# Layer 1 of a four-layer image network in one lane with fixed turns, beside the attention of layer 0

## The chip, the core and the metric

The kernel runs on one core of one Trainium2 chip. The core has five engines, each with its own queue that is worked off in order: PE (matrix products), DVE (vector arithmetic), ACT (activation functions and copies), POOL (a second, slower vector engine) and SP (which issues DMAs here). [...] The metric is the device time of one execution in microseconds (us), where lower is better.

## What is computed

Four layers follow each other on a batch of 4 images of 256 channels and 48 x 48 points (N = 2304). Each begins with a group norm of its input and adds its result to it:

```python
x = x + _L0_conv_ref(_gn(x), ...)   # attention: 8 heads of 64, q and k of length one
x = x + _L1_conv_ref(_gn(x), ...)   # a gate from a blurred, strip-convolved copy
x = x + _L2_conv_ref(_gn(x), ...)   # attention with one head of 64
x = x + _L3_conv_ref(_gn(x), ...)   # channel gate, 3 x 3 depthwise filter, norm
```

Layer 0 is the largest. Per image and head it forms `softmax(10 * q^T k) v` over 2304 x 2304 scores, then an output product. Layer 1 is small and has no large product:

```python
x_tem = _blur_pool(_max_pool_3x3(x), stride=3)          # 48 x 48 -> 16 x 16
s = x_h1 + x_w1 + x_h2 + x_w2                           # strip filters, 11 x 3 taps each
gate = jax.nn.sigmoid(batch_norm(s))
return x * gate[:, :, idx_h][:, :, :, idx_w]            # each gate value for 3 x 3 points
```

The four strip filters are summed into one filter per channel, whose taps the kernel lists in `TAPS`.

## The kernel before

**Tiling.** 256 channels are two tiles of 128 partitions (`k` = 0, 1; `NK` = 2). Heads are taken in pairs (`p` = 0 to 3). One head pair of one image is a phase: six units, each for 384 of the 2304 query points. A unit walks over the 18 blocks of 128 keys two at a time, so it has nine groups (`NG` = 9). The place of a group in its unit is called slot 0 to 8 below, so a phase has 54 groups and layer 0 has 16 phases, 864 groups. Layer 2 follows with 4 x 27 groups of the same kind, and layer 3 after them.

**One group.** `attend` (L382) writes the order of every engine by hand. For group t it emits: the scores of the two key blocks on PE and their exponentials on ACT (`scores`, L237 and L243; two PSUM tiles, so scores of one group need the exponentials of the one before); the sums of the exponentials of group t-1 on DVE and, for odd groups, first on POOL (`add_up`, L268, L277, L283); the jobs due in this group (`due`, then `fills`); the lanes, described below; and the value products of group t-1 on PE (`weigh`, L257). Eight buffers `pt` hold exponentials. A `pt` is free once `weigh` and `add_up` are done with it.

**What is due in a unit.** After the ninth group, in slot 0 of the next unit, `last` copies the result out of its single PSUM buffer (`take`, L330, ACT) and books the rest, counted in groups from there: the row sums (`total`, 3 groups on), a fold on POOL (2), the inverse of the sums with its DMAs (`invert`, L310 to L325, 6), the division on POOL (`divide`, L338, 10) and the output product with its addition to x (`out_proj`, L579 on PE, L584 on DVE, 11). Eleven groups on is slot 2 of the unit after. There a chunk of the next head pair's q, v and k is also made: in the order of PE, output product of the first channel half, q (L513), v (L529), k (L513), output product of the second half. They share two PSUM buffers `pj`. So v can start only when DVE has added the first output product to x, and k when ACT has moved q out. In groups 49, 51, 52 and 53 of a phase, DVE scales q for the next phase (L549 to L563).

**Layer 1 beside it.** For images 0 to 2 layer 1 runs in the phases of the next image (image b-1 beside image b), and for image 3 beside layer 2 (`l1_last`, which uses PE). Its work is a Python generator, `l1_all(b)` (L1011): group norm statistics (`gn`, L167); for each k the maxima and the blur (`maxima`, L666, six steps for each half image, DVE alone, L678 to L710); the padded tile (`padded`, L716, POOL, DVE and ACT); 19 rounds of products (`strips`, L728: four or five products on ACT, L741, and one sum on DVE, L759); the gate and its application (`gated`, L844, with POOL multiplications L867 and DVE additions L869); and the statistics for the norm of layer 2. Each `yield` ends one step. The number that it gives is how many groups to wait before the next.

A lane in `attend` spreads `n` steps evenly over its groups a to z, takes none in slot 0, and in its last group takes all that are left:

```python
until = -(-n * (st["at"] + 1 - a) // (z - a))
final = st["at"] == z - 1
while final or (done < until and t >= ready and not ends):
```

The generator is cut into four parts of 33 steps, one per phase (`part`, `L1_ALL`). The gate of k = 0 runs in a second list, `aside`, beside the maxima of k = 1.

Of the kernel before, what the change touches and what calls it, by code (L numbers as in the profile page):

```python
# [17 lines left out]
NK = 2  # L18
# [56 lines left out]
def usual_path(  # L75
# [88 lines left out]

    GN_TICKS = NSL + 4

    def gn(b, res, halves=range(NK)):  # L167

        if "st" not in res:
            res["st"] = small.tile([P, NK, NSL, 6], F32, tag="gn_st", name="gn_st")  # L170
        st = res["st"]
        for s in range(NSL if halves else 0):
            for k in halves:
                nc.vector.bn_stats(st[:, k, s, :], X[b][:, k, s * SL : (s + 1) * SL])
            yield 0
        mv = small.tile([P, NK, 2], F32, tag="gn_mv", name="gn_mv")
        for k in range(NK):
            nc.vector.bn_aggr(mv[:, k, :], st[:, k].rearrange("p s f -> p (s f)"))
        yield 3
        ps = pj_tile()  # L180
        nc.tensor.matmul(ps[:, 0:NK], lhsT=gmat, rhs=mv[:, :, 0], start=True, stop=True)
        gm = small.tile([P, NK], F32, tag="gn_gm", name="gn_gm")
        nc.vector.tensor_copy(gm, ps[:, 0:NK])
        dev = small.tile([P, NK], F32, tag="gn_dev", name="gn_dev")
        nc.vector.tensor_sub(dev, mv[:, :, 0], gm)
        sq = small.tile([P, NK], F32, tag="gn_sq", name="gn_sq")
        nc.vector.tensor_mul(sq, dev, dev)
        nc.vector.tensor_add(sq, sq, mv[:, :, 1])
        yield 2
        ps = pj_tile()  # L190
        nc.tensor.matmul(ps[:, 0:NK], lhsT=gmat, rhs=sq, start=True, stop=True)
        gv = small.tile([P, NK], F32, tag="gn_gv", name="gn_gv")
        nc.vector.tensor_scalar(gv, ps[:, 0:NK], GN_EPS, None, ALU.add)
        rs = small.tile([P, NK], F32, tag="gn_rs", name="gn_rs", bufs=6)
        rsqrt(rs, gv)
        yield 2
        nm = small.tile([P, NK], F32, tag="gn_nm", name="gn_nm", bufs=6)
        nc.vector.tensor_scalar(nm, gm, -1.0, None, ALU.mult)
        nb = small.tile([P, NK], F32, tag="gn_nb", name="gn_nb", bufs=6)
        nc.vector.tensor_mul(nb, nm, rs)  # L200
        res["rs"], res["nb"], res["nm"] = rs, nb, nm
        yield 1
# [153 lines left out]
        nc.vector.tensor_add(lsum[:, 0:1], lsum[:, 0:1], two[:, 0:1])  # L356
        nc.vector.tensor_tensor(lmin[:, 0:1], lmin[:, 0:1], two[:, 1:2], ALU.min)

    due, fills, aside, clock = {}, {}, [], {}
    AT_TOTAL, AT_FOLD, AT_INVERT, AT_DIVIDE, AT_AFTER = 3, 2, 6, 10, 11  # L360

    def last(u, t):

# [18 lines left out]
    def attend(phases):  # L382
# [16 lines left out]
        for t, (u, g, st) in enumerate(groups):  # L399
            for j in range(g * G, (g + 1) * G):  # L400
                scores(u, j)
            if prev is not None:
                add_up(*prev)
            do(due, t)
            do(fills, t)

            ends = prev is not None and prev[1] == NG - 1
            clock["t"] = t
            for lane in st["others"]:
                gen, n, a, z, done, ready = lane  # L410
                until = -(-n * (st["at"] + 1 - a) // (z - a))
                final = st["at"] == z - 1
                while final or (done < until and t >= ready and not ends):
                    wait = next(gen, None)
                    if wait is None:
                        break
                    done, ready = done + 1, t + wait
                    if final:
                        for other in list(aside):
                            if next(other[0], None) is None:  # L420
                                aside.remove(other)
                lane[4:] = done, ready
            for lane in list(aside):
                gen, ready = lane
                if t >= ready and not ends:
                    wait = next(gen, None)
                    if wait is None:
                        aside.remove(lane)
                    else:
                        lane[1] = t + max(wait, 1)  # L430
            st["at"] += 1
            if prev is not None:
                pu, pg = prev
                for j in range(pg * G, (pg + 1) * G):
                    weigh(pu, j)
                if pg == NG - 1:
                    last(pu, t)
            prev = (u, g)
# [220 lines left out]
        range(i, min(i + NT, len(TAPS))) for i in range(NT + 1, len(TAPS), NT)  # L659
    ]  # L660
    L1_BUF = (NT + 1) * AS * AS
    ROUND_TICKS = 2
    STRIP_TICKS = 2 * 6 + 2 + ROUND_TICKS * len(ROUNDS)
    GATE_TICKS = 7

    def maxima(b, k, res):  # L666

# [59 lines left out]

    def strips(b, k, norm, res):  # L728

        yield from maxima(b, k, res)  # L730
        pd = padded(k, norm, res)

        bufs = [
# [11 lines left out]
                )  # L745

        products(0)
        yield 2
        products(1)
        yield 2  # L750
        for n, taps in enumerate(ROUNDS):
            last = n == len(ROUNDS) - 1
            if n + 2 < len(ROUNDS):
# [5 lines left out]
            nc.vector.tensor_reduce(  # L759
                to, bufs[n % 3][:, :, : min(n, 1) + len(taps)], AX.X, ALU.add  # L760
            )

            for _ in range(ROUND_TICKS):
                yield 0

    TAPS_AT_ONCE = 12

# [242 lines left out]

    def l1_all(b):  # L1011

        yield from gn(b, norms1[b])
        res = {}
        yield from strips(b, 0, norms1[b], res)

        def rest():
            yield from gated(b, 0, norms1[b], res)
            norms2[b]["st"] = small.tile([P, NK, NSL, 6], F32, tag="gn_st2", name="gn_st2")
            for s in range(NSL):  # L1020
                nc.vector.bn_stats(
                    norms2[b]["st"][:, 0, s, :], X[b][:, 0, s * SL : (s + 1) * SL]
                )
                yield 1
            res["done"] = True

        aside.append([rest(), 0])
        one = {}
        yield from strips(b, 1, norms1[b], one)
        while "done" not in res:  # L1030
            yield 1
        yield from gated(b, 1, norms1[b], one)
        yield from gn(b, norms2[b], [1])

    def l1_last(b, ahead):

# [30 lines left out]
        def gates():  # L1067
            for k in range(NK):
                yield from until(res[k], "summed")
                yield from gated(b, k, norm, res[k])  # L1070
                yield from stats(k)
            yield from gn(b, norm2, [])

        return [ahead, tops(), sums(), gates()]

    L1_ALL = 2 * GN_TICKS + NK * STRIP_TICKS + GATE_TICKS
    l1 = [l1_all(b) for b in range(NX)]
    ahead = gn(B - 1, norms1[B - 1])
    lanes = l1_last(B - 1, ahead)

# [13 lines left out]
    def follow(start, slices, norm):  # L1094

        while "nb" not in norm:
            yield 1
        start()
        yield 1
        for c in range(L2C):  # L1100
# [28 lines left out]
    for i, (b, p) in enumerate(order):  # L1129
# [16 lines left out]
                work[NG * s + AT_CHUNK] = slices[s]  # L1146
        if (b, p) == (2, 0):
            for s in range(NSL):
                work.setdefault(s, []).append(lambda s=s: send(s))
                work.setdefault(s + 8, []).append(lambda s=s: receive(s))  # L1150
        if (b, p) == (0, 0):
            others.append((tap_weights(), WEIGHT_TICKS, 2, n - 2))
        if b > 0:
            ticks = -(-L1_ALL // NPAIR)
            first = AT_AFTER + 2 if p == 0 else 0
            others.append((part(l1[b - 1], ticks, p == NPAIR - 1), ticks, first, n - 2))
        if (b, p) == (B - 1, NPAIR - 1):
            others.append((part(ahead, L1_AHEAD, False), L1_AHEAD, n - L1_AHEAD - 3, n))
        if p == 1 and b + 1 < B:
# [1263 lines left out]
```

## The time and the profile before

| | |
|---|---|
| median of 10 runs | 3786.55 us (3781.2 to 3790.34) |
| the profiled execution: its own time | 3789.53 us |
| its span from first to last instruction | 3787.8 us |
| mean clock granted to PE | 0.967 of full speed |
| layer 0, image 0 (four phases, no layer 1 beside) | 52.7 to 761.6 us |
| layer 0, images 1 to 3 (layer 1 beside) | 761.6 to 3065.9 us |
| layer 2 | 3065.9 to 3516.8 us |
| layer 3 | 3516.8 to 3787.8 us |
| ACT exponentials L243, 1944 of them | 1477.1 us busy, 812 ns each |
| ACT products of layer 1, L741, 486 | 281.2 us, 752 ns each |
| DVE sums of layer 1, L759, 114 | 168.6 us, 1479 ns each |

The stages are cut at the first exponential of a phase. Busy time of an engine is the union or the sum of its instructions. A wait is put down to what ended it. The durations of a row are those of single instructions, which can overlap a little on one engine.

### The profile page before, as it was taken

What the parts mean: (1) busy time and instruction counts of PE and PEld (TensorE: products, weight loads), DVE (VectorE), ACT (ScalarE), POOL (GpSimd) and SP (SyncE); (2) the same over time, 40 slices, a digit from 0 to 9 for tenths busy, and PEclk for the clock granted to TensorE, in tenths of its full rate; (3) what the DMA queues carried; (4) which work ended last, traced back from release to release, by engine and by line L of the source; (5) the groups of instructions that cost most, each with busy time, mean ns of one, the idle gap of its engine ahead of it and who ended that gap; (6) DMA issues with size and microseconds to landing.
All of it is one profiled execution on the core that took longest, in us unless ns stands there. A gap on an engine that the chain in (4) does not pass through costs nothing.

```text
span 3787.8 us, 86425 instructions
## 1 busy us (share of the span) xinstructions
PE 3541.8 (94%) x36330; PEld 1797.1 (47%) x36330; DVE 2469.0 (65%) x3203; ACT 2360.3 (62%) x3819; POOL 1391.5 (37%) x900
## 2 busy tenths in 40 slices
PE   7999999998997999989979999899899999989685
PEld 4454555554443445544444445444444445655343
DVE  2455545566777666677686666766856677575687
ACT  5666666656774876658748766577487655555353
POOL 2333323332333333333333333333333356564242
PEclk9999999998998999999989999999899999999797
DMA  4111111110111111311111111111011100000001
GB/s 138 21 26 21 25 20 29 17 34 10 29 16 24 21 25 20 79 16 25 20 22 21 25 22 25 18 25 23 18 20 25 16 6 8 6 6 6 26 26 75
DMA packets 114591, 97.89 MB, mean 26 GB/s; under 512 B 56224, under 2 KB 111632, under 8 KB 112400
## 3 DMA queue, kind: packets, MB, share of 16 engines
q1 hardware_dynamic: 111728, 91.27, 12.7%
q8 instruction: 286, 4.69, 0.5%
q10 hardware_dynamic: 2464, 1.00, 0.1%
q14 instruction: 113, 0.93, 0.1%
HBM read 59.33 MB, written 11.80 MB: 19 GB/s over the span
## 4 chain that ended last, share of the span: by engine, by line
PE 69%; DVE 16%; ACT 7%; issue 5%; POOL 2%; DMA 1%; DVEq 0%; SPq 0%; ACTq 0%; POOLq 0%
PE sc L237 26%; PE av L257 25%; PE pj L513 6%; DVE acc L283 4%; PE pj L529 4%; PE pj L579 3%; ACT prod L741 3%; DVE sc L1413 2%; ACT pt L243 2%; DVE av L1413 1%; PE pj L290 1%; POOL half L268 1%; PE pj L805 1%; ACT row L299 1%; DVE acc L277 1%
## 5 line engine op out<-in xcount | busy, mean ns | idle before, releaser
L243 ACT ACTIVATE pt<-sc 128x768 f32<-128x768 f32 x1944 | 1477.1, 812 | 866.8 <-PE sc L237 863.3
L268 POOL TENSOR_TENSOR half<-pt 128x768 f32<-128x768 f32 x477 | 921.7, 1933 | 1818.5 <-ACT pt L243 1759.5
L237 PE MATMUL sc<-q,k 64*64 64x384 f32 x13824 | 1283.5, 486 | 36.0 <-DVE q L563 22.1
L257 PE MATMUL av<-pt,v 64*64 64x384 f32 x13824 | 1281.2, 486 | 0.0
L283 DVE TENSOR_TENSOR acc<-acc,pt 128x768 f32<-128x768 f32 x792 | 829.9, 1048 | 108.4 <-ACT pt L243 26.9
L237 PEld LDWEIGHTS sc<-q,k 64*64 64x64 f32 x13824 | 514.8, 133 | 661.3 <-issue 539.2
L257 PEld LDWEIGHTS av<-pt,v 64*64 64x64 f32 x13824 | 519.8, 133 | 588.9 <-issue 557.4
L283 DVE TENSOR_TENSOR acc<-acc,half 128x768 f32<-128x768 f32 x459 | 457.2, 996 | 416.5 <-POOL half L268 416.1
L584 DVE SCALAR_TENSOR_TENSOR x<-pj,bo,x 128x384 f32<-128x384 f32 x192 | 118.3, 617 | 564.1 <-PE pj L579 564.1
L513 PE MATMUL pj<-xs,w 128*128 128x384 f32 (+1 forms) x768 | 295.3, 510 | 2.3 <-issue 1.7
L741 ACT ACTIVATE prod<-pd,wt 128x256 f32<-128x256 f32 x486 | 281.2, 752 | 0.2
L338 POOL TENSOR_TENSOR o<-o,rinv 128x384 f32<-128x384 f32 x95 | 131.3, 1382 | 270.2 <-DMA rinv<-rinv 257.8
L529 PE MATMUL pj<-w,xs 128*128 128x128 f32 x1152 | 160.1, 293 | 41.1 <-DVE x L584 41.1
L579 PE MATMUL pj<-o,wo 128*128 128x384 f32 x384 | 169.2, 523 | 27.8 <-POOL o L338 22.9
L529 PEld LDWEIGHTS pj<-w,xs 128*128 128x128 f32 x1152 | 155.5, 207 | 75.0 <-DVE x L584 53.5
L513 PEld LDWEIGHTS pj<-xs,w 128*128 128x128 f32 x768 | 146.4, 202 | 85.7 <-issue 14.0
L257 PE MATMUL av<-pt,qv 64*64 64x384 f32 x1728 | 176.3, 502 | 0.0
L237 PE MATMUL sc<-qv,kd 64*64 64x384 f32 x1728 | 171.0, 490 | 3.9 <-ACT pt L243 3.9
L759 DVE TENSOR_REDUCE prod<-prod 128x256 f32<-128x1280 f32 x114 | 168.6, 1479 | 0.3
L277 DVE TENSOR_TENSOR acc<-pt 128x768 f32<-128x768 f32 x99 | 113.9, 1151 | 10.6 <-ACT pt L243 10.5
L579 PEld LDWEIGHTS pj<-o,wo 128*128 128x128 f32 x384 | 66.0, 193 | 112.7 <-issue 51.2
L330 ACT COPY raw<-av 128x768 f32<-128x768 f32 x108 | 86.3, 799 | 43.7 <-PE av L257 43.5
(226 smaller groups left out, 2696.9 us busy)
## 6 DMA issues: line engine op xcount, KB each, us to landing
xs<-in_x_dram SPq DMA_DIRECT2D x96, 384.0 KB
rinv<-rinv SPq DMA_DIRECT2D x208, 94.5 KB
x<-in_x_dram SPq DMA_DIRECT2D x6, 1152.0 KB
out_dram<-x SPq DMA_DIRECT2D x6, 1152.0 KB
l<-row SPq DMA_DIRECT2D x416, 1.5 KB
w<-in_wqkv_dram SPq DMA_DIRECT2D x32, 192.0 KB
rinv<-ls SPq DMA_DIRECT2D x208, 1.5 KB
x_out<-x SPq DMA_DIRECT2D x6, 384.0 KB
```

The costliest lines, as they stand in the source:

```text
L237: nc.tensor.matmul(ps[c * D : (c + 1) * D, h, :SL], lhsT=u["of"]["k"][r, j0 : j0 + D], rhs=u["of"]["q"][r, u["qc"]], start=True, stop=True,)
L243: nc.scalar.activation(pt, ps[:, :, :SL], AF.Exp, scale=u["scale"])
L257: nc.tensor.matmul(u["av"][h * D : (h + 1) * D, half, :SL], lhsT=value(u, j, h)[r], rhs=pt[r, h, :], start=j == 0, stop=j == JB - 1,)
L268: nc.gpsimd.tensor_add(half, pts[0], pts[1])
L277: nc.vector.tensor_add(u["acc"], ready[0], ready[1])
L283: nc.vector.tensor_add(u["acc"], u["acc"], term)
L338: eng.tensor_mul(o, o, u["rinv"])
L513: nc.tensor.matmul(ps[:, :n], lhsT=at["w"][:, k, t, :], rhs=xs[s][:, k, :n], start=k == 0, stop=k == NK - 1,)
L529: nc.tensor.matmul(ps[:, i * P : (i + 1) * P], lhsT=xs[s][:, k, i * P : (i + 1) * P], rhs=at["w"][:, k, 2, :], start=k == 0, stop=k == NK - 1,
L579: nc.tensor.matmul(ps[:, :SL], lhsT=wo[:, p, k * P : (k + 1) * P], rhs=o["o"], start=True, stop=True,)
L741: nc.scalar.activation(bufs[n % 3][:, :, min(n, 1) + i].rearrange("p (r c) -> p r c", c=AS), pd[:, PAD + dr : PAD + dr + AS, PAD + dc : PA ...
L759: nc.vector.tensor_reduce(to, bufs[n % 3][:, :, : min(n, 1) + len(taps)], AX.X, ALU.add)
```

## The change

Layer 1 of images 0 to 2 gets a fixed place in each unit. `paced` wraps the generator: it lets it take one step in slots 3, 5, 6 and 8 and two in slot 2, and none elsewhere. A step that says `ROUND` (a round of products) is followed by steps in slots 2, 5 and 8 alone; `HASTE` does the same with slots 2, 4, 6 and 8 and is used for image 2. The generator is no longer cut: it runs on over phases, and into the first 27 groups of the image after (`others.append((l1[b - 2], ..., 0, 3 * NG))`), beside the next image's own. Nothing is taken all at once in a phase's last group.

Within `l1_all` the order becomes serial: maxima, products and gate of k = 0, the statistics of k = 0, then the same for k = 1; the list `aside` goes. The first half of the maxima of k = 0 is taken before the norm's end. Between the blur and the padded tile at least three groups pass (`yield 3`). The rounds go on after the padded tile as before.

In layer 0 and layer 2, `invert` moves from 6 groups to 5 and `divide` from 10 to 9. The copy of image 0's x to memory and image 3's x into its place (`send`, `receive`) move from groups 0 to 5 and 8 to 13 of the phase to groups 18 to 23 and 36 to 41. `follow`, which starts the products of layer 2's last image, waits two groups more. The sums of `bn_stats` in `gn` yield after two slices where one channel half is taken. Layer 3 is as it was.

```diff
-    AT_TOTAL, AT_FOLD, AT_INVERT, AT_DIVIDE, AT_AFTER = 3, 2, 6, 10, 11
+    AT_TOTAL, AT_FOLD, AT_INVERT, AT_DIVIDE, AT_AFTER = 3, 2, 5, 9, 11
...
-            clock["t"] = t
+            clock["t"], clock["slot"] = t, st["at"] % NG
...
-                final = st["at"] == z - 1
+                clock["final"] = final = st["at"] == z - 1
...
+    TURNS, ROUND, HASTE = (2, 2, 3, 5, 6, 8), -1, -2
+    ROUND_TURNS = {ROUND: (2, 5, 8), HASTE: (2, 4, 6, 8)}
+
+    def paced(gen):
+
+        at, count, wait, turns = -9, 0, 0, TURNS
+        while True:
+            t, slot = clock["t"], clock["slot"]
+            count = count if t == at else 0
+            if not clock["final"] and (t < at + wait or count >= turns.count(slot)):
+                yield 1
+                continue
+            wait = next(gen, None)
+            if wait is None:
+                return
+            at, count = t, count + 1
+            turns = ROUND_TURNS.get(wait, TURNS)
+            yield 0
...
     def l1_all(b):
 
-        yield from gn(b, norms1[b])
+        norm, norm2 = norms1[b], norms2[b]
+        norm2["st"] = small.tile([P, NK, NSL, 6], F32, tag="gn_st2", name="gn_st2")
+        start = clock["t"]
+        ahead = gn(b, norm)
+        for _ in range(NSL - 1):
+            yield next(ahead)
         res = {}
-        yield from strips(b, 0, norms1[b], res)
...
+        tops = maxima(b, 0, res)
+        for _ in range(6):
+            yield next(tops)
+
+        while clock["t"] < start + NG + 2:
             yield 1
-        yield from gated(b, 1, norms1[b], one)
-        yield from gn(b, norms2[b], [1])
+        yield from ahead
+        yield from tops
+        for k in range(NK):
+            if k:
+                res = {}
+                yield from maxima(b, k, res)
+
+            yield 3
+            yield from strips(b, k, norm, res)
+            yield from gated(b, k, norm, res)
+            if k == 0:
+                for s in range(NSL):
+                    nc.vector.bn_stats(norm2["st"][:, k, s, :], X[b][:, k, s * SL : (s + 1) * SL])
+                    if s % 2:
+                        yield 0
+        yield from gn(b, norm2, [1])
...
         while "nb" not in norm:
             yield 1
+        yield 2
         start()
...
-                work.setdefault(s, []).append(lambda s=s: send(s))
-                work.setdefault(s + 8, []).append(lambda s=s: receive(s))
+                work.setdefault(s + 2 * NG, []).append(lambda s=s: send(s))
+                work.setdefault(s + 4 * NG, []).append(lambda s=s: receive(s))
...
         if b > 0:
-            ticks = -(-L1_ALL // NPAIR)
-            first = AT_AFTER + 2 if p == 0 else 0
-            others.append((part(l1[b - 1], ticks, p == NPAIR - 1), ticks, first, n - 2))
+            end = n - 2 if (b, p) == (B - 1, NPAIR - 1) else n + 1
+            others.append((l1[b - 1], 10**6, 2 if p == 0 else 0, end))
+        if b > 1 and p == 0:
+            others.append((l1[b - 2], 10**6, 0, 3 * NG))
```

## The prediction

> **What bounds the kernel now.** I read the page first, for the engine that carries the span.
>
> ```profile
> PE 3541.8 (94%) x36330; PEld 1797.1 (47%) x36330; DVE 2469.0 (65%) x3203; ACT 2360.3 (62%) x3819; POOL 1391.5 (37%) x900
> PE 69%; DVE 16%; ACT 7%; issue 5%; POOL 2%; DMA 1%; DVEq 0%; SPq 0%; ACTq 0%; POOLq 0%
> ```
>
> PE is busy nearly all the time, and 16% of the chain that ended last lies on DVE. Where, the table by stages tells; I cut it at the phases of layer 0. Columns: stretch, us, busy us of PE, PEld, DVE, ACT, POOL, PE's clock, DMA.
>
> ```profile
> 405.90:583.70 177.80, 177.75 (x1932) 89.56 (x1928) 90.57 (x122) 108.85 (x172) 57.95 (x38) 1.00 0.14 24
> 583.70:761.60 177.90, 177.85 (x1932) 89.57 (x1928) 95.37 (x123) 109.00 (x172) 57.97 (x38) 1.00 0.14 24
> 761.60:962.30 200.70, 188.94 (x1940) 93.99 (x1936) 133.97 (x176) 124.31 (x203) 66.32 (x40) 0.95 0.11 19
> 962.30:1152.30 190.00, 182.24 (x1936) 88.47 (x1932) 138.27 (x172) 135.61 (x226) 68.93 (x42) 0.98 0.13 22
> 1152.30:1353.50 201.20, 187.98 (x1932) 91.88 (x1928) 135.99 (x167) 138.53 (x230) 65.66 (x39) 0.96 0.14 24
> 1353.50:1534.20 180.70, 180.03 (x1940) 89.22 (x1936) 119.73 (x154) 121.49 (x198) 66.17 (x42) 1.00 0.14 24
> ```
>
> The first two rows are image 0, with no layer 1 beside: PE never idle, full clock, 177.85 us. The next four are image 1, the same PE work with layer 1 beside: PE is idle for 12, 8 and 13 us in three of them, and its clock falls with it. Images 2 and 3 repeat this (196.7, 189.5, 201.2, 180.8; 199.6, 187.9, 199.3). Yet DVE and ACT are at most 73% busy in any phase: this is a matter of order, not of capacity. Who stops PE there, the waits in that stretch tell (total, times, longest):
>
> ```profile
> PE pj L529 <- DVE x L584: 41.1, 14, 5.1
> PE pj L579 <- POOL o L338: 22.9, 11, 4.9
> PE sc L237 <- DVE q L563: 20.2, 3, 6.8
> PE sc L237 <- ACT pt L243: 11.6, 14, 1.9
> ```
>
> And the timeline shows how, DVE around one such wait:
>
> ```profile
> 1199.83 2.56 DVE L277 TENSOR_TENSOR acc<-pt 128x768 f32<-128x768 f32 x1
> 1202.31 1.50 DVE L703 TENSOR_TENSOR tf<-t 128x400 f32<-128x400 f32 x1
> ...
> 1205.59 0.29 DVE L710 SCALAR_TENSOR_TENSOR blur<-tf 128x128 f32<-128x128 f32 x1
> 1205.80 0.61 DVE L584 SCALAR_TENSOR_TENSOR x<-pj,bo,x 128x384 f32<-128x384 f32 x1
> ```
>
> L584 frees the PSUM buffer that v (L529) needs. It stood behind 3.4 us of maxima, put in slot 1, and a sum of exponentials that was late itself; PE stood for 5.1 us and then ran at half clock.
>
> **What the Trainium skill says.** "TensorE: Matmul & The Clock Gate", Part 1: PE's clock is halved after an idle window of about 3.4 us and comes back after a busy one. The trace agrees in kind: between 761 and 2890 us there are 17 half-clock stretches of 3.4 to 10.2 us, 122.9 us together, all behind gaps; but a gap of 1.9 us was enough for one. So an idle us costs more than itself: 98.1 us of idleness in these eleven phases came with 61.4 us of clock. "Perfetto Trace Analysis", DVE / Act Engine Instruction: the recorded time runs to the acknowledged write, so the records of neighbours overlap. Here four products of 745 ns took 2.1 us from start to start:
>
> ```profile
> 1047.22 2.32 ACT L741 ACTIVATE prod<-pd,wt 128x256 f32<-128x256 f32 x4
> 1049.32 1.56 ACT L243 ACTIVATE pt<-sc 128x768 f32<-128x768 f32 x2
> ```
>
> "SBUF — State Buffer", SBUF: two separate sides: a DVE operation with two SBUF inputs and one of POOL lock each other out for their whole length. It agrees with L681, 1.37 us at its fastest and 3.05 at its slowest; I use means, which hold this.
>
> **The change part by part.** *What can be won.* The eleven phases of images 1 to 3 (all but the very last) take 2889.2 - 761.6 = 2127.6 us; without layer 1 beside, 11 x 177.85 = 1956.4. The difference is 171.2. Group norm products on PE remain: the group with one takes 3.11 instead of 2.64 us, two per norm, eight norms: 8 us. So at most 163 can go. The last phase (176.7, with other products) I leave as it is: its idle time is six waits of 0.6 for ACT that the change doesn't touch.
>
> *Rounds in slots 2, 5, 8 (or 2, 4, 6, 8).* ACT per unit: 18 exponentials at 0.71 start to start 12.8, q, v, k 2.8, two rows 0.9, one copy 0.75: 17.2. Three rounds of 2.1 make 23.5, four 25.6; PE needs 29.65. After a round the next exponential starts 0.9 us late (the groups with a round are 3.48 instead of 2.59 from exponential to exponential), and a group's slack of about 1.15 takes that up by the second group. Before, rounds in slots 1, 3 and 6 did no harm: the row 1353.50 has rounds, and 0.7 us idle. New is slot 8, before the copy L330 of the single output buffer: PE waited up to 0.3 us for it, so over 38 units between 0 and 12 us. I take 0, as the copy ends about 0.2 us ahead; four rounds cost nothing either.
>
> *Gaps that go.* Maxima no longer stand in slots 0 and 1, ahead of L584: the waits L529 <- L584 and, since DVE held POOL's buffers and the inverse up, L579 <- L338 go in the main. No phase ends with all left-over steps at once: the three waits of 6.75 us for the scaling of q (L563) go.
>
> *What stays or comes, from DVE.* A step in slot 2 is written behind the second L584, which waits for PE's last product of the slot, about 7 us into it. So slot 2 hides little, and maxima start a third of a microsecond before slot 3. A full unit then has, one after the other: steps two and three 4.5 (L681, L682, L684, L688 by their means), sums of exponentials 3.2, step four 2.8, sums and inverse 3.7, step five 2.9, step six 1.4, sums 3.2, sums 3.4, a first sum 1.1, the first L584 0.6: 26.8. Slots 3 to 1 take 21.35, and v comes 3.6 after the start of slot 2: 24.95. With the 0.3 ahead, PE waits 26.5 - 24.95 = 1.6; 0.7 for clock: 2.3. As a check on the same addition, before 1196 us it gives 22.1 for a stretch that took 21.0. Seven such units in three images: 16. Two in which step one stood in slot 8 as well (2.2 more): 4.5 each, 9. In the first units of images 2 and 3 the rest of the image before shares the turns: some 5 us of statistics and additions come on top, and PE's small norm products wait for DVE too: 9.5 each, 19. Three lighter halves, 0.5 each: 1.5.
>
> *The padded tile.* In its slot ACT gets the tile (0.6) and five products behind POOL's memset (0.75) and a small DVE operation; three groups lie between it and the blur. I count exponentials 2.5 late against 1.0 allowed: 1.5 for the three k = 0, 0.2 for two k = 1 in slot 2, and 4 for image 2's second, followed by four more products in the next group: 9.
>
> *Sum of these:* 16 + 9 + 19 + 1.5 + 9 = 54.5, so layer 0 wins 163 - 55 = 108.
>
> *Inverse and division one group earlier.* In layer 0 neither engine has a sum between the old and the new place (add_up puts nothing on DVE in slot 6, nothing on POOL in slot 1), so only lane work is overtaken, and image 0 keeps its time. SP's DMAs follow at the same moment. In layer 2 DVE's inverse passes one sum; row copies and their DMA had landed by then. 0, between -3 and +3.
>
> *`follow`.* PE stood for the norm of the last image:
>
> ```profile
> 3393.97 0.98 PE L885 MATMUL pj<-gn_nb,w2c 128*128 128x1 f32 x4 [5.96 <-DVE gn_nb L200]
> ```
>
> Half clock followed for 6.8 us (3.4 lost). Two groups, over 5 us, cover nearly all; the chunks after it stay in their groups. 8 of 9.4.
>
> *send and receive* go to SP six times each, past fetches of x, in groups when image 0's x has been final for a group or more: nothing waits. The exchange is over before image 3's norm reads it, 19 groups later. 0.
>
> *Sum:* 108 + 8 = 116. The profiled execution took 3789.5: 3673.5. It lies 3 above the median, so **3670 us**.
>
> **The rivals.** *All is hidden.* DVE runs uncontended (maxima at their fastest, 1.4 for 1.9) and residual waits fall to 12: 3789.5 - 151 - 8 - 3 = 3627. For it: image 0, and that every gap has one of four causes, each addressed. Against: slot 2 is written behind L584. *DVE lag is passed on.* Each full unit leaves the next one behind, exponentials wait for `pt` as well, clocks halve: residual 100, 3715. For it: the lag of some 7 us before 1196. *Slower.* The round in slot 8 delays L330, and with one output buffer the value products stop in slot 1, in each of 38 units. To pass 3794 (0.2% above the median) it must eat 116 + 8 = 124 us, 3.3 a unit: more than a whole round of 2.1 laid bare. Priced with one whole round and half clock after it, 4 a unit, it gives 3670 + 152 = 3822. Waits for L330 of 0.3 at most speak against it. *The change doesn't do what it says:* rounds fit their turns (about 14 units per image and 24 to place them), so the end of a lane never flushes.
>
> **How the numbers follow.** Likeliest 3670: 0.65, its own range 3640 to 3700. All hidden 0.15, lag passed on 0.15, slower 0.04, no change 0.01. The range 3628 to 3710 reaches to both neighbours and takes in the bounds above. 0.2% is about what a measurement of this kernel tells from no change. Faster 0.95, same 0.01, slower 0.04.
>
> **What would show it.** By stages: phases of image 1 at 178 to 184 with clocks near 1.00; the first phases of images 2 and 3 longest. Waits L529 <- L584 down to a few of 2 us; no 6.8 for L563; L885 waiting under 1 us. Image 0 and layer 3 as before. I am wrong if PE idles in units that hold rounds alone, or waits for L330 by more than half a microsecond.

## The result, and the profile after

The changed kernel takes 3759.53 us (median of 8 runs, 3753.41 to 3761.68); the kernel before takes 3786.55 us (median of 28, 3779.23 to 3791.34). The ratio is 0.9928 with a 95% interval of 0.992 to 0.9937: 27 us faster, where 116 were forecast, and outside the range of 3628 to 3710. The profiled execution took 3769.65 us, its span is 3767.8. It is 10 us slower than the median, so what is read from this one profile below is known to some 10 us in all; by profiles the change won 20 us.

First the page of the changed kernel, the lines that answer to the two shown of before.

```profile
PE 3535.7 (94%) x36330; PEld 1782.4 (47%) x36330; DVE 2590.3 (69%) x3203; ACT 2359.4 (63%) x3819; POOL 1453.2 (39%) x900
PE 62%; DVE 25%; issue 5%; ACT 3%; POOL 2%; DMA 1%; SPq 0%; DVEq 0%; ACTq 0%; POOLq 0%
```

DVE has the same 3203 instructions, but is busy for 2590 us instead of 2469, and its share of the chain that ended last has grown from 16% to 25%. The same work takes DVE 121 us longer.

The table by stages, cut again at layer 0's phases (stretch, us, busy us of PE, PEld, DVE, ACT, POOL, PE's clock, DMA): one phase of image 0, the four of image 1, the last of image 3.

```profile
586.40:764.30 177.90, 177.85 (x1932) 89.55 (x1928) 93.50 (x122) 108.99 (x172) 58.03 (x38) 1.00 0.14 24
764.30:955.30 191.00, 182.98 (x1948) 90.78 (x1944) 142.04 (x175) 120.09 (x195) 69.59 (x40) 0.99 0.13 21
955.30:1142.10 186.80, 181.93 (x1924) 86.70 (x1920) 144.77 (x163) 138.72 (x233) 70.15 (x39) 1.00 0.14 23
1142.10:1336.70 194.60, 183.87 (x1944) 90.70 (x1940) 146.69 (x169) 122.88 (x199) 76.47 (x42) 0.98 0.13 22
1336.70:1518.50 181.80, 180.12 (x1927) 86.61 (x1920) 135.02 (x143) 137.32 (x231) 67.80 (x38) 1.00 0.14 24
...
2859.00:3045.90 186.90, 179.66 (x1908) 87.47 (x1904) 130.35 (x158) 114.42 (x175) 68.81 (x40) 0.95 0.13 21
```

Image 1 went from 200.7, 190.0, 201.2 and 180.7 to 191.0, 186.8, 194.6 and 181.8. The clock is nearly whole again (61 us were lost to it in the eleven phases of images 1 to 3, now 20), but PE's idle time in them fell only from 98 to 83 us. The very last phase went the other way, from 176.7 to 186.9. Layer 0 of images 1 to 3 as a whole: 2304.3 to 2281.6, 22.7 won where 108 were forecast.

PE's waits in that stretch (total, times, longest):

```profile
PE pj L518 <- DVE x L573: 55.8, 28, 4.5
PE sc L238 <- ACT pt L244: 9.8, 9, 2.2
PE pj L568 <- POOL o L339: 9.2, 10, 1.9
```

L518, L573, L568 and L339 are L529, L584, L579 and L338 of before. The wait of v for the first addition to x has not gone: 28 waits instead of 14, and 55.8 us instead of 41.1. The waits for the division are down from 22.9 to 9.2, the three of 6.8 for the scaling of q are gone.

To see what kind of unit pays, each unit of images 1 to 3 is taken from its slot 3 to the next slot 3, and the length of the same unit with no layer 1 (29.43 us, 30.06 in a phase's first and fifth, from image 0; 29.03 in the last phase) is taken off. The excess, by what layer 1 does in the unit, in us:

| unit holds | before | after |
|---|---|---|
| maxima | 136.6 in 15 (9.1 each) | 72.7 in 17 (4.3) |
| the padded tile | 15.9 in 6 | 14.0 in 6, three with maxima |
| rounds | 15.0 in 30 (0.50) | 32.0 in 31 (1.03) |
| a gate | 1.4 in 4 | 15.9 in 8 (2.0) |
| statistics only | 1.9 in 7 | 2.9 in 3 |
| the last phase, all six | 2.4 | 13.5 |
| sum | 173.3 | 151.1 |

A "bare" unit below is one of these lengths. The maxima paid 64 us less, as meant; rounds, gates and the last phase paid 43 us more.

### The profile page after: what moved, and what is told of

It is laid out like the page before. It is cut to its first block, busy times and chain, and to the rows that moved or that the text cites. A ratio compares the mean times of both kernels' runs of the same rounds, so it can differ in the third digit from the quotient of the medians.

```text
span 3767.8 us, 86478 instructions
## 1 busy us (share of the span) xinstructions
PE 3535.7 (94%) x36330; PEld 1782.4 (47%) x36330; DVE 2590.3 (69%) x3203; ACT 2359.4 (63%) x3819; POOL 1453.2 (39%) x900
## 4 chain that ended last, share of the span: by engine, by line
PE 62%; DVE 25%; issue 5%; ACT 3%; POOL 2%; DMA 1%; SPq 0%; DVEq 0%; ACTq 0%; POOLq 0%
PE av L258 23%; PE sc L238 23%; DVE acc L284 10%; PE pj L502 5%; PE pj L518 4%; PE pj L568 3%; DVE acc L278 2%; DVE sc L1426 2%; PE pj L291 1%; DVE av L1426 1%; ACT pt L244 1%; PE pj L809 1%; DVE gn_st L174 1%; ACT prod L747 1%; DVE x L573 1%
## 5 line engine op out<-in xcount | busy, mean ns | idle before, releaser
L269 POOL TENSOR_TENSOR half<-pt 128x768 f32<-128x768 f32 x477 | 961.4, 2017 | 1688.0 <-ACT pt L244 1619.0
L284 DVE TENSOR_TENSOR acc<-acc,pt 128x768 f32<-128x768 f32 x792 | 916.4, 1157 | 87.3 <-ACT pt L244 3.4
L284 DVE TENSOR_TENSOR acc<-acc,half 128x768 f32<-128x768 f32 x459 | 468.7, 1021 | 297.8 <-POOL half L269 295.7
L573 DVE SCALAR_TENSOR_TENSOR x<-pj,bo,x 128x384 f32<-128x384 f32 x192 | 118.1, 616 | 563.2 <-PE pj L568 563.2
L339 POOL TENSOR_TENSOR o<-o,rinv 128x384 f32<-128x384 f32 x95 | 128.4, 1352 | 303.9 <-DMA rinv<-rinv 286.7
L518 PE MATMUL pj<-w,xs 128*128 128x128 f32 x1152 | 155.9, 288 | 55.9 <-DVE x L573 55.8
L518 PEld LDWEIGHTS pj<-w,xs 128*128 128x128 f32 x1152 | 149.1, 201 | 92.3 <-DVE x L573 74.5
L568 PE MATMUL pj<-o,wo 128*128 128x384 f32 x384 | 167.7, 519 | 12.9 <-POOL o L339 9.2
L278 DVE TENSOR_TENSOR acc<-pt 128x768 f32<-128x768 f32 x99 | 140.9, 1423 | 18.6 <-ACT pt L244 18.6
L508 ACT ACTIVATE q<-pj,bias 128x384 f32<-128x384 f32 x96 | 55.7, 580 | 98.6 <-PE pj L502 97.9
L335 POOL TENSOR_TENSOR o<-raw 128x384 f32<-128x384 f32 x95 | 116.7, 1228 | 0.0
```

The costliest lines, as they stand in the source:

```text
L269: nc.gpsimd.tensor_add(half, pts[0], pts[1])
L278: nc.vector.tensor_add(u["acc"], ready[0], ready[1])
L284: nc.vector.tensor_add(u["acc"], u["acc"], term)
L518: nc.tensor.matmul(ps[:, i * P : (i + 1) * P], lhsT=xs[s][:, k, i * P : (i + 1) * P], rhs=at["w"][:, k, 2, :], start=k == 0, stop=k == NK - 1,
L568: nc.tensor.matmul(ps[:, :SL], lhsT=wo[:, p, k * P : (k + 1) * P], rhs=o["o"], start=True, stop=True,)
L573: nc.vector.scalar_tensor_tensor(xs, ps[:, :SL], pair["bo"][:, k : k + 1], xs, ALU.add, ALU.add)
```

## The experiments

All ratios are to the kernel before, run on the same chip at the same time (3787 to 3790 us in each set).

**Layer 1 left out.** How low can layer 0 go with this kernel's order?

```diff
     def l1_all(b):
-        norm, norm2 = norms1[b], norms2[b]
...
+        yield from gn(b, norms2[b])
```

> Layer 1 of images 0 to 2 is left out (only the norm statistics that layer 2 needs are kept), everything else as in the changed kernel. It shows the floor under which no placing of layer 1 can go. Theory A (all of the loss in the phases of images 1 to 3 comes from layer 1's work): these phases fall to 178 to 179 us each, no clock loss there, and the time is about 3760 - 151 = 3610 us. Rival (the earlier inverse and division, or the moved copies of image 0, cost by themselves): phases stay above 181 us, 3640 us or more.

3621.86 us (a single run). The phases of images 1 to 3 take 177.2 to 179.5 us each, the very last 174.5, and no clock is lost. Their units are 5.4 us above bare in all; 4.8 of that is in the five norms that this kernel keeps, 0.95 each. So nearly all of the excess is layer 1's. This is the floor; that the work could be hidden down to it is not shown.

**Other turns for the rounds.**

```diff
-    ROUND_TURNS = {ROUND: (2, 5, 8), HASTE: (2, 4, 6, 8)}
+    ROUND_TURNS = {ROUND: (1, 3, 6), HASTE: (1, 3, 6, 8)}
```

> Rounds of products in slots 1, 3, 6 (image 2: 1, 3, 6, 8) instead of 2, 5, 8 (2, 4, 6, 8); all else as in the changed kernel. In the changed kernel a unit with rounds alone is 1.0 us above one without layer 1, before it was 0.5. Theory R (the slots of the rounds matter, above all slot 2 behind the products of q, v, k and slot 8 ahead of the copy of the output buffer): 31 units win 0.5 us each and the last phase some 8, 3735 to 3745 us. Rival D (what is lost in these units is the late addition to x, by DVE's own lag, whatever the slots of ACT's products): 3755 to 3765 us.

3749.18 us, ratio 0.99 (0.9883 to 0.9917). Units with rounds fall from 1.03 to 0.68 each, the last phase from 13.5 to 9.3. The turns cost some 10 us by medians, between the two ranges expected.

**Slot 2: the lanes ahead of the second output product.** In slot 2 the jobs that follow k, the second output product with its addition among them, are written after the lanes' steps instead of before them, in layer 0 alone.

```diff
-            for _, fn in sorted(jobs, key=lambda job: job[0]):
+            for at, fn in sorted(jobs, key=lambda job: job[0]):
+                if late is not None and at >= 4:
+                    late.append(fn)
+                    continue
                 fn()
...
-            do(fills, t)
+            late = []
+            do(fills, t, late if st["at"] % NG == 2 and len(u["of"]) and "shift" not in u["of"] else None)
...
+            for fn in late:
+                fn()
```

> In slot 2 of layer 0 the lane's steps are written ahead of the second output product and its addition to x, so that DVE has them while PE makes v and k; all else as in the changed kernel. Theory A (DVE's lag: in slot 2 it stands still for 4 us behind PE's last product and does the maxima after that): units with maxima, 4.3 us above the floor each, lose half of it, and the 20 of them win 35 to 50 us: 3710 to 3725 us. Rival B (POOL, by the division that waits for its DMA and by the shared port, holds DVE up in slots 0 and 1): under 10 us, 3750 to 3762.

3698.56 us, ratio 0.9757 (0.9741 to 0.9773): 61 us below the changed kernel. Units with maxima go from 4.3 to 2.0 each, rounds from 1.03 to 0.63, gates from 15.9 to 10.9 in all, the last phase from 13.5 to 4.0. Everything that layer 1 does profits, not the maxima alone, and more than expected. First the timeline of DVE in one slot 2 of the changed kernel, from the second addition on (start, us, line, shapes, idle before and releaser; L686 is a step of the maxima):

```profile
1217.05 0.62 DVE L573 SCALAR_TENSOR_TENSOR x<-pj,bo,x 128x384 f32<-128x384 f32 x1 [3.95 <-PE pj L568]
1217.59 1.37 DVE L686 TENSOR_TENSOR t<-t 128x1175 f32<-128x1175 f32 x1
```

and the same place with the lanes ahead (L573 is L579 here, L686 is L692, and L695 is the next step):

```profile
1202.28 0.62 DVE L579 SCALAR_TENSOR_TENSOR x<-pj,bo,x 128x384 f32<-128x384 f32 x1 [2.69 <-PE pj L574]
1202.81 1.38 DVE L692 TENSOR_TENSOR t<-t 128x1175 f32<-128x1175 f32 x1
...
1204.32 1.36 DVE L695 TENSOR_TENSOR t<-t 128x1152 f32<-128x1152 f32 x1
1206.84 0.62 DVE L579 SCALAR_TENSOR_TENSOR x<-pj,bo,x 128x384 f32<-128x384 f32 x1 [1.17 <-PE pj L574]
```

Between the two additions PE makes q, v and k. In the changed kernel DVE stands still there for 3.95 us and the maxima start behind the second addition. With the lanes ahead, 2.9 us of maxima lie in that hole, and 1.17 us of waiting are left.

**Inverse and division at their old places.**

```diff
-    AT_TOTAL, AT_FOLD, AT_INVERT, AT_DIVIDE, AT_AFTER = 3, 2, 5, 9, 11
+    AT_TOTAL, AT_FOLD, AT_INVERT, AT_DIVIDE, AT_AFTER = 3, 2, 6, 10, 11
```

> Inverse and division back at 6 and 10 groups, all else as in the changed kernel. If the earlier places cost nothing and win nothing (as predicted): 3757 to 3763 us. If the earlier inverse helps because it is ahead of slot 5's lane step: slower by 10 to 30 us, 3770 to 3790. If the earlier division blocks POOL and so DVE: faster by 10 us or more, below 3750.

3752.58 us, ratio 0.9903 (0.9887 to 0.992), against 0.992 to 0.9937 of the changed kernel: at most a few us are to be had. Rounds fall to 0.62 each, though nothing was done to them, and maxima rise to 4.65.

**Which half of a round costs?** One kernel without DVE's sums of the products (but the last of each strip), one without ACT's products (but the first three rounds).

```diff
-            nc.vector.tensor_reduce(
-                to, bufs[n % 3][:, :, : min(n, 1) + len(taps)], AX.X, ALU.add
-            )
+            if last:
+                nc.vector.tensor_reduce(
+                    to, bufs[n % 3][:, :, 1 : 1 + len(taps)], AX.X, ALU.add
+                )
```

> The changed kernel, but the sums of a strip's products on DVE (TENSOR_REDUCE, 120 in all, 114 of them beside layer 0) are left out, all but the last of each strip, so the gate is computed from a part of the taps. ACT's products stay. In the changed kernel a unit that holds rounds alone takes 1.03 us more than one with no layer 1, 32 us over 31 such units. If this comes from DVE (a sum of 1.48 us written in slot 2 behind the second addition to x, so in the way of what follows), the excess falls below 0.3 us a unit and the time to 3725 to 3740. If it comes from ACT (a round of 2.1 us ahead of the next exponential), 0.7 us or more of it stays and the time is 3750 or above.

3734.44 us, ratio 0.9858 (0.9842 to 0.9874). That is in the range expected if DVE's sums are the cost. The 31 units that hold rounds in the changed kernel take 14.4 us over bare units here, 32.0 there.

```diff
-            if n + 2 < len(ROUNDS):
+            if n + 2 < 3:
                 products(n + 2)
```

> The changed kernel, but ACT makes the products of the first three of a strip's 19 rounds alone; the sums on DVE all stay and read what these left, so the gate is computed from a part of the taps. The mirror of the kernel without sums. If DVE's sums make the cost of the rounds, 0.7 us or more a unit of the 1.03 stays and the time is 3745 or above; if ACT's products do, the excess falls below 0.3 us and the time to 3725 to 3740. If both kernels keep half of it each, the two engines' delays add up (ACT late gives DVE's sums late).

3750.67 us, ratio 0.9896 (0.988 to 0.9913), rounds 0.88 each. The mean of 1.03 us hides three kinds of units (us over bare, all of a kind together):

| units with rounds | changed | without sums | without products |
|---|---|---|---|
| the 6 directly behind a unit with a padded tile | 13.2 | 3.1 | 9.6 |
| the 10 beside the norm of the next image | 13.2 | 5.8 | 17.5 |
| the other 15 | 5.6 | 5.6 | 0.3 |

In the 15, where DVE has nothing else of layer 1 or of a norm to do, its sums cost nothing and ACT's products all of the 0.4 us a unit. In the 16 others, where DVE is late from maxima or has statistics beside, the sums carry 17.5 us. Taking the products out won nothing there (27.1 against 26.4; that profile is 9 us above its kernel's median and has four units of 3.2 to 4.1, so the comparison is rough). Of the 32.0 us, then, 17.5 are DVE's sums, 1.9 the norm's small products on PE, and what is left is 0.4 a unit, as in the 15. The prediction had looked at ACT alone.

How can a sum of 1.48 us hurt, when DVE is idle a quarter of the phase? It shows in the lengths of DVE's other operations. The groups of instructions by line and form, in the last phase of image 1, which holds rounds and little else, first in the kernel with layer 1 left out (busy us, mean ns, then the idle time before):

```profile
L284 DVE TENSOR_TENSOR acc<-acc,pt 128x768 f32<-128x768 f32 x48 | 49.2, 1025 | 5.4 <-DVE acc L284 0.5
L311 DVE TENSOR_TENSOR ls<-l 128x6 f32<-128x6 f32 x6 | 1.0, 158 | 0.0
```

in the changed kernel:

```profile
L284 DVE TENSOR_TENSOR acc<-acc,pt 128x768 f32<-128x768 f32 x48 | 56.0, 1167 | 5.4 <-ACT pt L244 0.5
L311 DVE TENSOR_TENSOR ls<-l 128x6 f32<-128x6 f32 x6 | 7.5, 1248 | 0.0
```

and with the lanes ahead in slot 2:

```profile
L284 DVE TENSOR_TENSOR acc<-acc,pt 128x768 f32<-128x768 f32 x48 | 48.2, 1005 | 5.4 <-ACT prod L753 0.5
L311 DVE TENSOR_TENSOR ls<-l 128x6 f32<-128x6 f32 x6 | 0.9, 158 | 0.0
```

L311 is an addition of six numbers per partition: 158 ns alone, 1248 ns on average where DVE comes late, with no wait before it. What it runs into is POOL: of the 104 such additions in the changed kernel's whole trace 31 took more than 0.4 us, and every one of the 31 ended 20 to 26 ns after an operation of POOL did. In the kernel before there were 10 such, with the lanes ahead 20, with layer 1 left out 4, all with the same end.

A stretched operation costs nothing by itself. In this very phase the first five units, of rounds alone, take 2.0 us over bare in the changed kernel, 2.1 with the lanes ahead, where L311 is short, and 1.9 without sums. It costs where PE waits for what comes behind. The timeline of the changed kernel shows such a place beside a norm, round the step from one unit to the next:

```profile
1039.88 2.63 POOL L269 TENSOR_TENSOR half<-pt 128x768 f32<-128x768 f32 x1 [3.05 <-ACT pt L244]
...
1052.27 1.53 POOL L339 TENSOR_TENSOR o<-o,rinv 128x384 f32<-128x384 f32 x1 [4.39 <-DMA w<-in_wqkv_dram]
1053.76 2.52 POOL L269 TENSOR_TENSOR half<-pt 128x768 f32<-128x768 f32 x1
1056.24 1.71 POOL L335 TENSOR_TENSOR o<-raw 128x384 f32<-128x384 f32 x1
```

```profile
1040.75 1.79 DVE L311 TENSOR_TENSOR ls<-l 128x6 f32<-128x6 f32 x1
...
1054.54 2.56 DVE L278 TENSOR_TENSOR acc<-pt 128x768 f32<-128x768 f32 x1
1057.02 0.60 DVE L573 SCALAR_TENSOR_TENSOR x<-pj,bo,x 128x384 f32<-128x384 f32 x1
```

The inverse (L311) stands for POOL's half, from 1040.75 to its end at 1042.5. The division L339 then waits 4.39 us for a DMA to land, so that half and fold come directly behind it and run to 1057.95; the first sum L278 lies beside both and takes 2.56 us for 1.04; the addition L573 comes at 1057.02, and v stood for 0.69 us. A round's sum does not overload DVE here: it shifts DVE's short operations into POOL's, and the addition to x comes late. Over images 1 to 3 (764 to 2976 us) L284 with two exponentials, L278 and L311 took 1051, 1179 and 313 ns in the kernel before and 1210, 1604 and 757 in the changed one; with the counts of 557, 70 and 69 that is 149 us more of DVE's time for the same work; some other operations took less.

**All three edits together.**

> All three edits together: in slot 2 the lanes ahead of the second output product, rounds in slots 1, 3, 6 (1, 3, 6, 8 for image 2), invert and divide back at 6 and 10 groups. The first alone gave 3698.6 us, the second won 10, the third 7. If the three act on different waits, their gains add up: 3680 to 3688. If they all relieve the same lag of DVE and POOL in the units with rounds (1.03 us a unit, which each of them alone brought to 0.62 to 0.68), the second and third bring little on top: 3692 to 3700.

3696.28 us (3693.41 to 3697.47), ratio 0.9756 (0.974 to 0.9772): no different from slot 2 alone. The time is that of the second expectation, but it is a sum of two things: maxima fall from 2.0 to 1.5 each and the padded tile from 11.0 to 7.1 in all, while the eight units with a gate rise from 10.9 to 26.4. So it does not show that the edits relieve the same lag.

**One step less per unit.** On the kernel with all three edits:

```diff
-    TURNS, ROUND, HASTE = (2, 2, 3, 5, 6, 8), -1, -2
+    TURNS, ROUND, HASTE = (2, 2, 5, 6, 8), -1, -2
```

> The kernel with all three edits, and one step of a unit fewer: turns in slots 2, 2, 5, 6, 8, none in slot 3. Maxima then take 5 units per channel half instead of 4. If a unit's cost is a threshold (what DVE can't take up within a unit), a smaller load falls below it and the 34 us of the units with maxima shrink to 20 to 25: 10 us below the kernel with all three. If each step costs what it costs wherever it stands, the sum is the same and the time within 3 us of that kernel.

3701.89 us, ratio 0.977 (0.9754 to 0.9786), 6 us above that kernel: both expectations missed. Yet the units show the threshold that the first one looked for. Nine units that hold maxima in both kernels, away from the start of an image, took 15.7 us over bare with six steps, and take 0.9 with five, eight of them nothing at all. But the lane became longer, and at the start of images 2 and 3 it runs beside the next one, with much of a gate: the first three units of these images rise from 11.0 to 33.4 us. The padded tile rises from 7.1 to 10.4.

**No step in slot 2.** On the changed kernel:

```diff
-    TURNS, ROUND, HASTE = (2, 2, 3, 5, 6, 8), -1, -2
+    TURNS, ROUND, HASTE = (3, 3, 5, 6, 8, 8), -1, -2
```

> The changed kernel, with the two steps of slot 2 put into slots 3 and 8: turns 3, 3, 5, 6, 8, 8, the same number of steps per unit, none behind the second output product in slot 2. The rounds keep theirs. In the changed kernel DVE stands still some 4 us in slot 2 before that product and the two steps come after. If only this loss of 4 us counts (the hole is used by neither kernel), the 73 us of the units with maxima stay and the time is 3752 to 3768. If the two steps do harm as they stand ahead of the sums of slot 3 and of the inverse, so that POOL's division is late, the units with maxima fall to 40 to 55 us and the time to 3728 to 3745.

3779.87 us, ratio 0.9978 (0.9969 to 0.9988): slower than either expectation, 20 us above the changed kernel. Maxima cost 6.4 us a unit. Two steps in slot 2 were therefore not the worst place, even behind the second addition. A likely reason, not tested alone, is that a step late in the unit (slot 8) has less time to be made up before v needs the addition.

**The gate in slots of its own.** On the kernel with the lanes ahead in slot 2. In the next two kernels the later gate of image 0 runs on into groups 22 and 23, while image 0's x is copied to memory in groups 18 to 23, so layer 2 of image 0 works on slices that lack the last of that gate.

```diff
-    ROUND_TURNS = {ROUND: (2, 5, 8), HASTE: (2, 4, 6, 8)}
+    ROUND_TURNS = {ROUND: (2, 5, 8), HASTE: (2, 4, 6, 8), GATE: (4, 6, 8)}
...
+        slow = GATE if b < NX else 1
...
-        yield 1
+        yield slow
```

> The kernel with the lanes ahead of the second output product in slot 2 (3698.6 us), and the steps of the gate in slots 4, 6, 8 alone, one each, instead of two in slot 2 and one in 3, 5, 6, 8. In that kernel the five units with most of a gate are the longest of all: 4.3, 6.7, 2.7, 5.2 and 1.9 us over a unit without layer 1, two of them with statistics besides. If it is the packing (POOL's multiplications of 2.1 us, one behind the other with halves, fold and division), the gate spread over three units costs at most 0.7 a unit and the time is 3684 to 3690. If each multiplication costs about 1 us wherever it stands, it is the same sum over more units: 3695 to 3702.

3718.63 us, ratio 0.9815 (0.9799 to 0.9832).

> As the kernel with the gate in slots 4, 6, 8, but in slots 3, 5, 7, where POOL has no sum to make and DVE has three. If POOL's multiplications do harm as they lock DVE out (a sum of 0.96 us becomes 2.0 to 2.6 beside them), this is slower than slots 4, 6, 8 by 3 us or more. If they do harm as they delay POOL's own sums and the division, it is the same or faster by up to 4 us.

3711.09 us (3707.42 to 3721.18), ratio 0.9803 (0.9785 to 0.9821). Both lost 12 to 20 us, for a reason that no expectation had: the lane of images 0 and 1 now ended late in the next image, and its last steps, the norm for layer 2, were all taken at the end of its 27 groups. PE's waits in the second kernel:

```profile
PE pj L182 <- DVE gn_mv L179: 18.7, 2, 16.3
PE pj L524 <- DVE x L579: 16.4, 11, 3.3
```

A wait of 16.3 us for one small matrix product of that norm. The unit lengths answer the question all the same. The two units with the gate of the first channel half beside image 1 take 34.34 and 29.43 us where it is packed, 30.07 and 30.09 in slots 4, 6, 8, and 30.06 and 29.43 in slots 3, 5, 7, which is what they take bare; the same gate beside image 3 took 34.22 us in its second unit in slots 4, 6, 8, and 29.45 in slots 3, 5, 7. So packing does most of the harm, POOL's own sums in the even slots some, and a multiplication beside DVE's sums none that reaches PE.

**The first gate alone moved, to slots 1, 3, 5, 7,** so that the lane ends in time:

```diff
-        slow = GATE if b < NX else 1
+        slow = GATE if b < NX and (k == 0 or b == NX - 1) else 1
```

> The kernel with the lanes ahead of the second output product in slot 2 (3698.6 us), and the gate of the first channel half (and image 2's second) in slots 1, 3, 5, 7, where POOL has no sum of its own; the gate of images 0 and 1's second half stays as it was there, so that the lane still ends within the first 27 groups. In slots 3, 5, 7 the two units with a first gate took 30.06 and 29.43 us, as without layer 1; packed they took 34.3 and 29.4. If POOL's even slots are the cause, the units of image 1 and 2 (4.3 and 2.7) and image 2's last (1.9 and some 2 in the last phase) go: 3686 to 3692. If slot 1 puts a multiplication ahead of fold and half in slot 2 and so delays the second next output product, half of it or all comes back: 3693 to 3702.

3709.77 us, ratio 0.9801 (0.9787 to 0.9814): slower than with the gate left alone (0.9741 to 0.9773), and than both expectations. The gates did go down (7.2 us in ten units), but of the two units with a multiplication in slot 1 one still took 34.6 us (the other 31.0), and the steps behind the gate moved by a few slots: units with maxima took 47.5 us in 15 instead of 34.0 in 17. The fastest kernels remain the ones with slot 2 reordered, 3696 to 3699 us, 2.4% below the kernel before.

## Why the prediction was wrong, step by step

**What could be won: right.** The ceiling of 163 us, and the rival "all is hidden" at 3627, meet the kernel with layer 1 left out, 3621.86. The 8 us for the products of eight norms come out too: that kernel keeps five norms, at 0.95 each.

**Rounds: the step that failed outright.** "Before, rounds in slots 1, 3 and 6 did no harm", and so slots 2, 5, 8 "I take 0". They cost 32.0 us, 1.03 in each of 31 units, 17 more than before. Already the reading was wrong: the row 1353.50 is idle for 0.7 us, but 2.8 us longer than 177.85 (a norm's products are 1 of it), and rounds paid 0.50 a unit before. The step counted ACT's products and their room before the next exponential, and asked what slot 8 does to the copy L330; it never asked where DVE's sum of each round falls. The products cost 0.4 a unit after all, shown in the 15 units where nothing else of layer 1 stands; the sums cost 17.5 us, all of it in the 16 units where DVE has other work or comes late from the maxima. There PE was idle for 13.4 us. In the 15 units that hold rounds alone it was idle for 0.3: the sign that the prediction named came only where rounds have company.

**The gate: not costed.** But for the additions at the start of images 2 and 3 it was in no term of the sum; packed into six turns a unit it took 15.9 us. Its place alone, slots 3, 5, 7, brought the first gate's units back to their bare length.

**Units with maxima: right mechanism, too small.** The prediction saw that slot 2 "is written behind the second L584" and hides little, and put 2.3, 4.5 and 9.5 us on such units, 0.5 on three light halves: 45.5 in fourteen. Fourteen such units (all but three that hold a first step and little else) measured 71.6, or 5.1 each. The term for DVE's work was near: 26.8 by means, and 27.6 measured from the end of a second addition to the end of the next first one, over twelve such units in which DVE waited for nothing but PE's output products. The room was right too: 24.95, against 24.9 in most units without layer 1. But the stretch took 29.0 us, as 0.3 of waiting and 1.1 between DVE's records, with no wait recorded, come on top: 4.1 us beyond the room, where 1.6 was counted. The padded tile, 9, measured 14.0 together with the maxima in three of its six units.

**The last phase "I leave as it is": wrong, 10.2 us.** Its lane ends there, and its beginning shows one chain, in the timeline of the changed kernel:

```profile
2862.61 4.06 DVE L284 TENSOR_TENSOR acc<-acc,pt 128x768 f32<-128x768 f32 x2
...
2866.60 1.75 DVE L278 TENSOR_TENSOR acc<-pt 128x768 f32<-128x768 f32 x1
...
2868.26 0.15 DVE L900 TENSOR_TENSOR bias<-pj,b2c 128x2 f32<-128x2 f32 x1
...
2868.51 2.26 PE L925 MATMUL pj<-xs,w 128*128 128x384 f32 x3 [2.56 <-issue]
```

The bias for layer 2's first image stands behind sums that were themselves late; PE idled for 2.56 us before its products, which began 0.1 us after the bias, and 10.2 us at half clock followed. A packed gate at 2937 us took another 4.9. With slot 2 reordered the phase took 177.4.

**`follow`, "8 of 9.4": wrong, about 1.** The wait for the norm went, as forecast, but another took its place:

```profile
3371.89 1.73 DVE L201 TENSOR_TENSOR gn_nb<-gn_nm,gn_rs 128x2 f32<-128x2 f32 x1
...
3376.90 1.76 DVE L311 TENSOR_TENSOR ls<-l 128x6 f32<-128x6 f32 x1
...
3378.91 1.02 DVE L981 BATCH_NORM_STATS2 bst<-pj 128x6 f32<-128x384 f32 x2
```

```profile
3379.53 0.76 PE L889 MATMUL pj<-gn_nb,w2c 128*128 128x1 f32 x4 [3.18 <-DVE bst L981]
```

The norm (L201) was done 5.9 us before PE's products (L889) began. They waited for DVE's statistics (L981) of an earlier product in the buffers `pj`, which stood behind late sums and an inverse (L311) of 1.76 us. So PE idled for 3.18 us instead of 5.96, and for 1.04 in the products ahead, with half clock for 6.8 us as before. That stage of layer 2 went from 114.0 to 113.1.

**Inverse and division, 0 within 3:** undone, they gave 7 us by medians, but the intervals touch; no more can be said. **`send` and `receive`, 0**, and layer 3 (271.0 to 270.1): as forecast.

Together: the eleven phases came out 75 above the forecast (rounds 32, gates 16, maxima and padded tile 87 for 54.5, statistics 3, less the norm's 8 counted among them), the last phase 10, `follow` 7. 3673.5 + 92 = 3765.5, against the profiled 3769.65. The rival "DVE lag is passed on" (3715) had the mechanism, as far as any had, with the wrong reach: the lag is passed on in light units too, as the six behind a padded tile show (13.2 us; the six behind one before had 0.9).

What stays open: what the 1.1 us between DVE's records in a full unit is made of, and why the gates become dearer with all three edits. Two units make most of that, the beginnings of a second gate: 1.6 and 1.9 us in the changed kernel, 6.5 and 6.9 with all three edits. With the other turns for the rounds alone both take 5.4, with the old inverse and division alone 1.9 and 5.2, so either edit has a part in it. How far the 10 us between this profile and the median lie in single units is not known.

## What to carry over

When work is laid beside a critical engine, cost every instruction of a step on every engine it goes to, and ask of each in whose shadow its place puts it; a short operation that comes late can take several times its length, on an engine that is idle a quarter of the time. Then ask who waits for what comes behind it: where nobody did, the stretching cost nothing. Split a mean by what else a unit holds before giving it a cause; here one of 1.03 us was three different things. Look for holes that the schedule makes by itself (here 3.9 us between two additions that wait for PE), and write the side work into the hole, before the instruction that ends it. A lane that must be done by a fixed group has to be counted to its end whenever a turn is changed: fewer steps a unit made the units with maxima nearly free and lost it again where two lanes met.

## What the runs showed of the hardware

The addition of six numbers took 158 ns and, beside an operation of POOL, up to 1.8 us; a sum of 0.96 us took 2.56. The Trainium skill's "SBUF — State Buffer", section "SBUF: two separate sides", cited in the prediction, has the lock between a DVE operation with two inputs and one of POOL, and the ends that fall together (31 of 31) agree with it. That it can fall on the smallest operation, for as long as POOL's still runs, and is written into its duration and not as a wait, is what the list of waits hides. It is seen by comparing one line's mean between two kernels.

The length of a half-clock stretch doesn't follow the gap. In layer 0 beside layer 1 the two kernels have 29 of them, each 3.4, 6.8 or 10.2 us long. In the changed kernel 2.56 us of idleness at 2866 us brought 10.2 us of it, one of 3.28 at 1244 us brought 6.8, two of 2.43 and 2.44 at 1943 and 2961 us brought 3.4 and 6.8, while gaps of 1.87 and 1.62 us at 1178 and 1182 brought none.
